# Layer 2's one-hots by nodes: four comparisons with a number per partition in place of one comparison of two tensors

## The chip, the cores and the metric

The kernel runs on one core of one Trainium2 chip. The metric is the time of one execution on the device in microseconds (us), the median over several runs. The engines of the core work side by side, each through its own queue in order: TensorE (PE; its weight loads are listed as PEld), VectorE (DVE), ScalarE (ACT), GpSimd (POOL) and SyncE (SP). They wait for each other through semaphores.

## The reference

A graph network of four layers over 12,500 nodes with 96 features and 200,000 edges sorted by destination. Each layer is added to its input and normalised. The change concerns layer 2, attention along the edges:

```python
Q_h = (x @ Wq + bq).reshape(N, H, D)          # H = 8 heads of D = 12
K_h = (x @ Wk + bk).reshape(N, H, D)
V_h = (x @ Wv + bv).reshape(N, H, D)
E = (edge_attr @ We + be).reshape(-1, H, D)
score = K_h[src_idx] * Q_h[dst_idx] / jnp.sqrt(jnp.asarray(D, x.dtype)) * E
score = jnp.exp(jnp.clip(score.sum(-1, keepdims=True), -5.0, 5.0))
msg = V_h[src_idx] * score
wV = jax.ops.segment_sum(msg, dst_idx, num_segments=N)
Z = jax.ops.segment_sum(score, dst_idx, num_segments=N)
h_out = wV / (Z + 1e-06)
...
x = _layernorm(x + h_out.reshape(N, H * D))
```

The two segment sums are what the changed lines serve: each edge's message and weight are added to the row of its destination node.

## The kernel before, in words

`passes()` does layers 0 and 1, `attention()` does layer 2, and a last `whole_pass` does layer 3, one after the other. Layer 3 reads a table of layer 2's result (`ex_d`, and `kept[2]` on the chip), so it starts when layer 2 has ended.

In `attention()` the 200,000 edges are 1563 tiles of 128 edges, an edge per partition. Four tiles are a unit (`UE` = 4), so there are 391 units, the last one of three tiles. Nodes are grouped in 98 windows of 128. Because edges are sorted by destination, a tile's edges fall into two neighbouring windows, `nominal(t)` and the next one; `by_columns` computes for each edge its node's place in these two windows, a number from 1 to 256 (`within`, one column per tile, lines 570 to 583).

Per unit the kernel does the following.

- `ask(u)`, line 1536: GpSimd issues four indirect DMAs, one per tile, that gather for each of 128 edges the row of K and V of its source (`kv_d`, 192 f32) into `kv`, a ring of 12 buffers. It is called 8 units ahead (`EARLY`). The indices are a column of `cols` on the chip. In what follows, "a gather" is one of these instructions.
- `queries(u)`, lines 1563 and 1564: ScalarE makes the one-hots that pick the destination's Q row.
- `score(u)`: TensorE multiplies the edge attributes by We (`ep`, line 1574) and picks Q (`qp`, line 1578). VectorE forms the products (1582, 1583), sums over each head (1585) and clips (1586).
- `weigh` and `terms`: ScalarE takes the exponential (1594, 1596), VectorE multiplies V by it (1597), and both split the f32 message into two f16 halves (1606 and 1607, tile `mh`).
- `one_hots_of(u)`, line 1613: VectorE compares `wide`, a table of the numbers 1 to 256 with each number repeated four times, with `within`, and so makes for the four tiles of the unit the 128 x 256 one-hot that says which edge goes to which node (`ohe`, bf16). The layout is node first, tile last: `ohe[p, node, tile]`.
- `scatter(u, m, ohe)`, line 1629: for each tile and each of its two windows TensorE multiplies a 128 x 128 slice of `ohe` as weights by the 208 columns of `mh` and accumulates in PSUM. When a window is complete, `done` (lines 1642 to 1647) divides by the sums, and after four windows a `stage` (lines 1655 to 1698) normalises the nodes and writes layer 3's table, a few instructions per unit.

The order on PE, DVE, ACT and POOL in this stage is the order in which the code calls these functions (`manual_schedule`): in the loop's turn u the score of unit u, the weighing of u - 1, the splitting and the one-hots of u - 2, the scatter of u - 3. On VectorE a turn is thus 1582, 1583, 1585, 1586, 1597, 1607, 1613, then the `done` and `stage` instructions that are due. Line 1613 waits for nothing but a free buffer; the next instruction, line 1582 of the following unit, waits for that unit's four gathers and for `ep`.

In layers 0 and 1 other lines are of use as a measure: 1013 is a VectorE comparison of a bf16 row with a number per partition, 1311 an indirect DMA of GpSimd like that of line 1536, 1018 a scan along a row.

Of the kernel before, what the change touches and what calls it, by code (L numbers as in the profile page):

```python
# [11 lines left out]
F32 = mybir.dt.float32  # L12
BF16 = mybir.dt.bfloat16
# [3 lines left out]
ALU = mybir.AluOpType  # L17
# [6 lines left out]
P = 128  # L24
# [496 lines left out]
NT = (E + P - 1) // P  # L521
# [20 lines left out]
def gnn_fast(  # L542
# [4 lines left out]
    nc = tc.nc  # L547
# [19 lines left out]
    nc.vector.memset(eps, LN_EPS)  # L567


    def by_columns(pool, t0, t1):  # L570

        cols = pool.tile([P, t1 - t0], I32, name="cols")
        nc.sync.dma_start(cols, cols_src[:, t0:t1])
        within = pool.tile([P, t1 - t0], BF16, name="within")
        with tc.tile_pool(name="n_work", bufs=1) as work:
            dst_i = work.tile([P, t1 - t0], I32, name="dst_i")
            nc.scalar.dma_start(dst_i, cols_dst[:, t0:t1])
            nom = work.tile([P, t1 - t0], I32, name="nom")
            nc.gpsimd.iota(nom, pattern=[[1, t1 - t0]], base=t0 + 8, channel_multiplier=0)
            nc.vector.tensor_scalar(nom, nom, 4, None, op0=ALU.arith_shift_right)  # L580
            nc.vector.tensor_scalar(nom, nom, P, -P - 1, op0=ALU.mult, op1=ALU.add)
            nc.vector.tensor_sub(within, dst_i, nom)
        return cols, within

    def without_slots(pool, ns):

        t0 = 16 * ns - 8
        src_, in_0 = by_columns(pool, t0, NT)
        in_1 = pool.tile([P, NT - t0], BF16, name="in_1")
        nc.vector.tensor_scalar(in_1, in_0, float(-P), None, op0=ALU.add)  # L590
        return ns, t0, src_, (in_0, in_1)
# [44 lines left out]
    with tc.tile_pool(name="w_work", bufs=2) as work, tc.tile_pool(name="w_psum", bufs=2, space=PSUM) as psum:  # L636
        for i in range(DEPTH):
            t = const.tile([D + 1, 2 * D], F32, name=f"w_l1_{i}")
# [72 lines left out]
    for i in range(2):  # L711
        t = const.tile([D + 1, GB, P], F32, name=f"aug{i}")
# [115 lines left out]
    def nominal(t):  # L828
        return (t // 8 + 1) // 2 - 1
# [666 lines left out]
    def attention():  # L1496
        H1 = HD + 1
        W = HEADS * H1
        per = UE
        EARLY = 8  # L1500
        with ExitStack() as c2:
            cols, within = by_columns(c2.enter_context(tc.tile_pool(name="e_cols", bufs=1)), 0, NT)
            work = c2.enter_context(tc.tile_pool(name="e_work", bufs=3))
            uw = c2.enter_context(tc.tile_pool(name="e_unit", bufs=3))
            one = c2.enter_context(tc.tile_pool(name="e_one", bufs=1))
# [1 line left out]
            accp = c2.enter_context(tc.tile_pool(name="e_acc", bufs=3, space=PSUM))  # L1507
            five = one.tile([P, per, HEADS], F32, name="five")
            nc.vector.memset(five, 5.0)
            wide = one.tile([P, 2 * P, per], BF16, name="wide")  # L1510
            nc.gpsimd.iota(
                wide, pattern=[[1, 2 * P], [0, per]], base=1, channel_multiplier=0, allow_small_or_imprecise_dtypes=True
            )
            attr = []
            for i in range(6):
                t = one.tile([D + 1, per * P], F32, name=f"attr{i}")
# [3 lines left out]
            blocks, got, asked, early, acc, held = {}, {}, {}, {}, {}, {}  # L1520
# [88 lines left out]

            def one_hots_of(u):  # L1610
                t0, n = units[u]
                o = uw.tile([P, 2 * P, per], BF16, name="ohe")
                nc.vector.tensor_tensor(  # L1613
                    o[:, :, :n], wide[:, :, :n], within[:, None, t0 : t0 + n].to_broadcast([P, 2 * P, n]), op=ALU.is_equal
                )
                return o

            def scatter(u, m, ohe):
                t0, n = units[u]
                for i in range(n):  # L1620
                    t = t0 + i
                    for k in range(2):
                        d = nominal(t) + k
                        if not 0 <= d < NB:
                            continue
                        first, last = max(0, 16 * d - 8), min(NT - 1, 16 * d + 23)
                        if t == first:
                            acc[d] = accp.tile([P, 2, W], F32, name="acc")
                        nc.tensor.matmul(  # L1629
                            acc[d].rearrange("p t w -> p (t w)"), ohe[:, k * P : (k + 1) * P, i],  # L1630
                            m[:, i].rearrange("p t w -> p (t w)"), start=(t == first), stop=(t == last),
                        )
                        if t == last:
                            done(d, acc.pop(d))

            def done(d, a):
                g = d - d % GB
                n = min(GB, NB - g)
                if d == g:
                    held["y"] = one.tile([P, GB, D], F32, name="y")  # L1640
                s = uw.tile([P, W], F32, name="both")
                nc.vector.tensor_reduce(s, a.rearrange("p t w -> p w t"), AX.X, ALU.add)
                sh = s.rearrange("p (h d) -> p h d", d=H1)
                z = uw.tile([P, HEADS, 1], F32, name="z")
                nc.vector.tensor_scalar(z, sh[:, :, HD:], 2.0**-8, 1e-6, op0=ALU.mult, op1=ALU.add)
                nc.vector.reciprocal(z, z)
                nc.vector.tensor_mul(
                    held["y"][:, d - g, :].rearrange("p (h d) -> p h d", d=HD), sh[:, :, :HD], z.to_broadcast([P, HEADS, HD])
                )
                if d == g + n - 1:  # L1650
                    stages.append(stage(g, n, held.pop("y")))
# [53 lines left out]
            with tc.manual_schedule(engines={ET.PE, ET.DVE, ET.Activation, ET.Pool}):  # L1705
                for u in range(EARLY):
                    ask(u)
                for u in range(3):
                    queries(u)
                for u in range(len(units) + 3):  # L1710
                    ask(u + EARLY)
                    fetch(u + 4)
                    if u < len(units):
                        steps[0].append(score(u))
                    if 1 <= u < len(units) + 1:
                        steps[1].append(weigh(*steps[0].pop(0)))
                    if 2 <= u < len(units) + 2:
                        steps[2].append((terms(*steps[1].pop(0)), one_hots_of(u - 2)))
                    queries(u + 3)
                    if stages and next(stages[0], stages) is stages:  # L1720
                        stages.pop(0)
                    if u > 2:
                        scatter(u - 3, *steps[2].pop(0))
                for st in stages:
                    for _ in st:
                        pass
# [90 lines left out]
    with tc.tile_pool(name="h_tab", bufs=1) as pool:  # L1817
        kept[2] = new_table(pool, 4 * D, F16)
        at_3 = without_slots(pool, NS3)
        attention()  # L1820
        whole_pass(
            at_3, ex_d, in_batches(l3_stage, terms=(2, 1, 1)), in_batches(l3_stage, terms=(2, 1, 1), name="sums_e"),
            kept[2][1],
        )


    with tc.tile_pool(name="f_work", bufs=1) as work, tc.tile_pool(name="f_psum", bufs=1, space=PSUM) as psum:
        t = work.tile([P, 1], F32, name="found")
# [3 lines left out]
        p = psum.tile([1, 1], F32, name="p")  # L1832
# [59 lines left out]
```

## Time and profile before

| | us |
|---|---|
| median of 3 runs | 5880.89 |
| lowest and highest run | 5874.62, 5888.94 |
| the profiled execution | 5885.37 |
| its span, first to last instruction | 5883.6 |
| layer 2, 2895 to 4993 | 2098 |
| layers 0 and 1, before it | 2895 |
| layer 3, after it | 891 |

| busy us in the span | PE | PEld | DVE | ACT | POOL |
|---|---|---|---|---|---|
| whole | 4446.7 | 3267.7 | 4378.5 | 2718.9 | 4095.9 |
| layer 2 | 1409.8 | 1276.9 | 1564.1 | 1012.2 | 1591.0 |

Durations are from the one profiled execution. A group of instructions is named by its line, its engine and its operation, then the tile that it writes and those that it reads, with the number of times, the busy time, the mean of one in ns, and how long its engine had been idle before it, with what ended that. "issue" means that nothing the profile shows was waited for. Two instructions of VectorE that follow each other without a wait overlap in these records by about 80 ns, so what one costs its queue is the distance between two starts.

### The profile page before, as it was taken

To read this page: it belongs to the slowest core of one execution; us is meant where nothing else is said; L and a number is where in the kernel's file an instruction comes from. 1 tells how busy PE (TensorE), PEld (TensorE's weight loads), DVE (VectorE), ACT (ScalarE), POOL (GpSimd) and SP (SyncE) were. 2 spreads that over 40 slices of the span, in tenths; PEclk is the share of its full clock that TensorE was granted. 3 is DMA by queue.
4 is the path that set the end of the run, shared out by engine and by line. 5 is a ranking of instruction groups with operands and counts; after the bars stand their busy time and mean duration, and the time that the engine had idled before them with its cause. 6 is when DMAs were issued, how large, how long until landed. Compare 5 with 4: busy or idle time off the path is not lost. (4 is left out here: it accounts for less than half of the span.)

```text
span 5883.6 us, 131235 instructions
## 1 busy us (share of the span) xinstructions
PE 4446.7 (76%) x51487; PEld 3267.7 (56%) x51487; DVE 4378.5 (74%) x9063; ACT 2718.9 (46%) x5380; POOL 4095.9 (70%) x3648
## 2 busy tenths in 40 slices
PE   4667777777778987898666667666666765899998
PEld 3444444554456765666566566666666664445454
DVE  7589899998746665776677777777777777577776
ACT  1445444444534443555444444444444444444444
POOL 0267677767667775777477777777777776777773
PEclk7576767776779998999755655555556566899999
DMA  3555555555556665776555555555555554555553
GB/s 100 156 156 184 172 170 173 164 166 166 179 149 167 171 160 140 190 193 187 150 152 155 157 156 156 156 156 155 156 153 156 155 157 131 137 145 151 146 151 88
DMA packets 671708, 920.46 MB, mean 156 GB/s; under 512 B 399034, under 2 KB 465293, under 8 KB 671077
## 3 DMA queue, kind: packets, MB, share of 16 engines
q1 hardware_dynamic: 502198, 621.59, 33.7%
q0 software_dynamic: 150624, 283.99, 20.8%
q10 hardware_dynamic: 18255, 6.39, 0.5%
q8 instruction: 406, 6.65, 0.5%
q14 instruction: 225, 1.84, 0.1%
HBM read 778.75 MB, written 132.81 MB: 155 GB/s over the span
## 5 line engine op out<-in xcount | busy, mean ns | idle before, releaser
L1311 POOL DMA_INDIRECT rows_e<-tab_d,cols x1257 | 1658.3, 1319 | 423.7 <-issue 292.9
L1536 POOL DMA_INDIRECT kv<-kv_d,cols x1563 | 1590.9, 1018 | 485.4 <-issue 382.0
L1369 ACT CAST msg<-rows 128x768 f16<-128x768 f32 (+1 forms) x1320 | 796.9, 640 | 853.8 <-PE rows L1366 832.8
L1629 PE MATMUL acc<-mh,ohe 128*128 128x208 f16 x3115 | 566.7, 355 | 661.3 <-DVE ohe L1613 653.8
L1369 DVE CAST msg<-rows 128x768 f16<-128x768 f32 x660 | 630.0, 955 | 369.5 <-PE rows L1366 363.6
L1629 PEld LDWEIGHTS <-ohe 128*128 128x128 bf16 x3115 | 379.3, 137 | 781.8 <-DVE ohe L1613 738.4
L1366 PE MATMUL rows<-tab,ohT 128*32 128x192 f16 (+1 forms) x19992 | 763.8, 277 | 56.0 <-ACT msg L1369 21.7
L1311 POOL DMA_INDIRECT rows_e<-ex_d,cols x611 | 592.2, 969 | 186.2 <-issue 154.2
L1375 PE MATMUL acc<-msg,ohd 128*128 128x192 f16 (+1 forms) x5100 | 693.7, 276 | 1.6 <-issue 1.6
L1574 PE MATMUL ep<-w_e,attr 97*128 97x96 f32 x3126 | 689.7, 396 | 5.0 <-DVE s L1582 4.2
L1574 PEld LDWEIGHTS ep<-w_e,attr 97*128 97x128 f32 x3126 | 660.4, 310 | 14.1 <-DVE s L1582 4.6
L1366 PEld LDWEIGHTS <-ohT 128*32 128x32 fp8e4 x19992 | 425.5, 97 | 350.8 <-issue 298.5
L1297 PE MATMUL acc<-rows_e,ones_e 128*128 128x192 f16 (+2 forms) x3660 | 493.3, 285 | 93.8 <-DMA rows_e<-tab_d,cols 51.2
L1582 DVE TENSOR_TENSOR s<-ep,kv 128x384 f32<-128x384 f32 x391 | 217.6, 556 | 442.8 <-DMA kv<-kv_d,cols 358.9
L1594 ACT ACTIVATE ex<-sc 128x32 f32<-128x32 f32 x391 | 89.6, 229 | 984.8 <-DVE sc L1586 951.8
L1375 PEld LDWEIGHTS <-ohd 128*128 128x128 fp8e4 x5100 | 407.0, 99 | 233.4 <-issue 179.3
L1235 ACT CAST msg<-rows 128x768 f16<-128x768 f32 x600 | 366.0, 641 | 319.0 <-PE rows L1231 293.0
L1297 PEld LDWEIGHTS <-ones_e 128*128 128x128 bf16 x3660 | 365.2, 117 | 187.9 <-issue 93.9
L1244 PE MATMUL acc<-msg,ohd 128*128 128x193 f16 x1800 | 305.1, 295 | 112.8 <-ACT msg L1235 100.6
L1231 PE MATMUL rows<-tab,ohT 128*32 128x192 f16 x7056 | 332.2, 294 | 49.6 <-ACT msg L1235 20.0
L1175 POOL DMA_INDIRECT spare<-tab_d,spare_i x72 | 141.5, 1966 | 317.8 <-DMA rowd<-lorow 134.9
L1018 DVE TENSOR_TENSOR_SCAN cnt<-cb,run,sb 128x2048 bf16<-128x2048 bf16 (+1 forms) x73 | 324.3, 4443 | 4.6 <-DMA cb<-crow 4.6
(701 smaller groups left out, 7577.7 us busy)
## 6 DMA issues: line engine op xcount, KB each, us to landing
ohT<-ohT_d SPq DMA_DIRECT2D x204, 400.0 KB
ohd<-ohd_d SPq DMA_DIRECT2D x204, 400.0 KB
attr<-cols_edge_attr_dram SPq DMA_DIRECT2D x390, 192.0 KB
bc<-rowd SPq DMA_DIRECT2D x72, 800.0 KB
qb<-qrow SPq DMA_DIRECT2D x97, 512.0 KB
sb<-srow SPq DMA_DIRECT2D x72, 512.0 KB
cb<-crow SPq DMA_DIRECT2D x72, 512.0 KB
ohd_d<-ohd SPq DMA_DIRECT2D x72, 400.0 KB
```

Of the source, the lines that this page charges most:

```text
L1018: nc.vector.tensor_tensor_scan(cnt[:, : n * P], cb[:, : n * P], sb[:, : n * P], c.run, op0=ALU.mult, op1=ALU.add)
L1231: nc.tensor.matmul(ps[j * GR : (j + 1) * GR, i // R, i % R * W : (i % R + 1) * W], a, b, start=True, stop=True)
L1235: nc.scalar.copy(m[:, : n * R, :W].rearrange("p (b r) w -> p b r w", r=R), ps[:, :n, : R * W].rearrange("p b (r w) -> p b r w", r=R),)
L1244: nc.tensor.matmul(acc[d][:, : W + 1], got[d][1][:, q, :], m, start=(q == 0), stop=(q == SQ - 1))
L1297: nc.tensor.matmul(acc[:, : W + count], ones[:, :, i], rows_of[u][:, i, : W + count], start=(t + i == first), stop=(t + i == last),)
L1311: nc.gpsimd.indirect_dma_start(out=m[:, i, :W], out_offset=None, in_=table, in_offset=bass.IndirectOffsetOnAxis(ap=rest_src[:, t : t + 1], ...
L1366: nc.tensor.matmul(ps[j * GR : (j + 1) * GR, i // R, i % R * W : (i % R + 1) * W], a, b, start=True, stop=True)
L1369: (nc.scalar.copy if engine else nc.vector.tensor_copy)(m, ps[:, :, : R * W])
L1375: nc.tensor.matmul(acc[d][:, :W], got[d][1][:, q, :], m, start=(q == 0), stop=(q == SQ - 1))
L1536: nc.gpsimd.indirect_dma_start(out=kv[:, i, :], out_offset=None, in_=kv_d, in_offset=bass.IndirectOffsetOnAxis(ap=cols[:, t0 + i : t0 + i ...
L1574: nc.tensor.matmul(ep[:, i, :], a[:, i * P : (i + 1) * P], w_e, start=True, stop=True)
L1629: nc.tensor.matmul(acc[d].rearrange("p t w -> p (t w)"), ohe[:, k * P : (k + 1) * P, i], m[:, i].rearrange("p t w -> p (t w)"), start=(t = ...
```

## The change

The one-hots of a unit are made by four instructions, one per tile, each comparing the table with one number per partition, the tile's column of `within`. The table holds each number once, the layout of `ohe` is tile first and node last, and `scatter` takes its weights from adjacent columns. `within` is kept in f32 in this layer. On TensorE's queue each tile's first weight load now waits for that tile's comparison; on the others the order is the same, but for a load of the node stage (`x_in`) that moves by a few places on SP's queue.

```diff
-    def by_columns(pool, t0, t1):
+    def by_columns(pool, t0, t1, dtype=BF16):
...
-        within = pool.tile([P, t1 - t0], BF16, name="within")
+        within = pool.tile([P, t1 - t0], dtype, name="within")
...
-            cols, within = by_columns(c2.enter_context(tc.tile_pool(name="e_cols", bufs=1)), 0, NT)
+            cols, within = by_columns(c2.enter_context(tc.tile_pool(name="e_cols", bufs=1)), 0, NT, F32)
...
-            wide = one.tile([P, 2 * P, per], BF16, name="wide")
-            nc.gpsimd.iota(
-                wide, pattern=[[1, 2 * P], [0, per]], base=1, channel_multiplier=0, allow_small_or_imprecise_dtypes=True
-            )
+            wide = one.tile([P, 2 * P], BF16, name="wide")
+            nc.gpsimd.iota(wide, pattern=[[1, 2 * P]], base=1, channel_multiplier=0, allow_small_or_imprecise_dtypes=True)
...
-                o = uw.tile([P, 2 * P, per], BF16, name="ohe")
-                nc.vector.tensor_tensor(
-                    o[:, :, :n], wide[:, :, :n], within[:, None, t0 : t0 + n].to_broadcast([P, 2 * P, n]), op=ALU.is_equal
-                )
+                o = uw.tile([P, per, 2 * P], BF16, name="ohe")
+                for i in range(n):
+                    nc.vector.tensor_scalar(o[:, i], wide, within[:, t0 + i : t0 + i + 1], None, op0=ALU.is_equal)
...
-                            acc[d].rearrange("p t w -> p (t w)"), ohe[:, k * P : (k + 1) * P, i],
+                            acc[d].rearrange("p t w -> p (t w)"), ohe[:, i, k * P : (k + 1) * P],
```

## The prediction

> **What bounds the kernel now.** I read the page first, for the whole; then the busy time by stage, to find the stage of the change; then the gathers' own line, for what their engine waits for; then the timeline, instruction by instruction.
>
> From the page, the costliest groups (count, busy us, mean ns, then the engine's idle time before them and what ended it):
>
> ```profile
> L1536 POOL DMA_INDIRECT kv<-kv_d,cols x1563 | 1590.9, 1018 | 485.4 <-issue 382.0
> ...
> L1629 PE MATMUL acc<-mh,ohe 128*128 128x208 f16 x3115 | 566.7, 355 | 661.3 <-DVE ohe L1613 653.8
> ...
> L1582 DVE TENSOR_TENSOR s<-ep,kv 128x384 f32<-128x384 f32 x391 | 217.6, 556 | 442.8 <-DMA kv<-kv_d,cols 358.9
> ```
>
> TensorE waits 654 us for the one-hots of L1613, which looks like the bound. It is not: VectorE, which makes them, itself stood idle 443 us at L1582, the first instruction of each unit, mostly for the gathered rows. The gathers are GpSimd's. Stage by stage (PE, PEld, DVE, ACT, POOL busy us, clock, DMA share, GB/s):
>
> ```profile
> 2895.00:4993.00 2098.00, 1409.80 (x9379) 1276.86 (x9380) 1564.11 (x3433) 1012.21 (x2131) 1590.95 (x1563) 0.59 0.56 155
> ```
>
> From the source view of the gathers' line:
>
> ```profile
> L1536 POOL DMA_INDIRECT kv<-kv_d,cols x1563: 942/949/1477, 2901.2 to 4967.4; - x196
> ...
>   issue: 382.0, 1253
>   DVE ohe L1613: 56.7, 186
> ```
>
> The first gather starts at 2901.2 and the last at 4967.4. 1590.9 us busy plus 1562 gaps of 0.305 us (382.0/1253, and 56.7/186 for those put down to L1613: the same length, so no real wait) is 1590.9 + 476 = 2067, which is that whole stretch. GpSimd issues gathers back to back and never waits for a buffer: it is the bound of this stage, at 4 x (1.018 + 0.305) = 5.29 us per unit.
>
> A gather usually takes 946 ns; the mean is 1018. The excess, 1563 x 72 ns = 113 us, is what can be won or lost here. The timeline shows it:
>
> ```profile
> 4006.12 0.58 DVE L1607 TENSOR_TENSOR mh<-m,mh 128x416 f16<-128x416 f32 x1
> 4006.62 0.69 DVE L1613 TENSOR_TENSOR ohe<-wide,within 128x1024 bf16<-128x1024 bf16 x1
> ...
> 4006.68 1.45 POOL L1536 DMA_INDIRECT kv<-kv_d,cols  x1 [0.30 <-issue]
> 4008.43 0.95 POOL L1536 DMA_INDIRECT kv<-kv_d,cols  x1 [0.30 <-issue]
> ```
>
> The gather that starts 60 ns into L1613 takes 1.45 us instead of 0.95. I set each of the 1563 gathers against the VectorE instruction running 34 ns after its start. With a comparison or product of two SBUF tensors there, the gather is longer by the rest of that instruction less 90 ns: for L1613, 103 gathers, 398 ns each measured and 398 by the rule; L1597, 180 of 206 (rule 207); L1607, 77 of 257 (rule 257). With nothing or a PSUM-fed instruction there, 711 gathers and more, about 2 ns. So L1613 costs 103 x 398 = 40.9 us, L1597 37.0, L1607 19.8, the node stage's lines the rest.
>
> **What the Trainium skill says.** "SBUF — State Buffer", Who interferes with whom: VectorE and GpSimd share one pair of SBUF ports; a VectorE instruction with two SBUF inputs collides with GpSimd's reads, one in a two-port mode with reads and writes. The trace agrees on reads (above). It says that the loser blocks for the whole instruction; here L1613 runs 675 to 739 ns beside gathers of 945, so it doesn't wait them out, and the measurement decides. "VectorE: DVE Perf Modes", The perf-mode tier table: bf16 tensor_scalar gets the fourfold, two-port mode, tensor_tensor twofold. The trace agrees: L1013, the same form as the new comparison (bf16, is_equal, a number per partition), takes 740 ns for 2048 elements, L1613 682 for 1024.
>
> **The change part by part.**
>
> *VectorE's time.* L1613 occupies the queue for about 600 ns (L1607 to L1613 is 502 ns apart for 416 elements, so 69 ns over one element per cycle at 0.96 GHz; 1024 at two per cycle is 533 + 67). A comparison of 256 elements: L1013's pair at 1150.82 starts 660 ns apart, 533 of it stream, so 127 fixed. L1053, with a number per partition, is 162 apart from its follower, and L1064, with a constant, 102: 60 ns are the scalar's. So 256/4/0.96 = 67 + 127 = 194 ns, four are 776: 176 ns more per unit.
>
> *Waits of VectorE for a gather.* L1661, a two-port instruction of 4 elements, takes 168 ns alone and 385 when it starts 555 ns after a gather; all such end about 940 ns after the gather's start. The gather thus holds the ports from about 590 to 840 ns. Four comparisons of 776 ns against 1250 ns of cycle: 0.2 x 125 + 0.62 x 250 = 180, and 20 for the gather's brief read: 0.2 us per unit. Together 0.38 us more per unit; VectorE is idle 1.13 us per unit at L1582 (442.8/391), so GpSimd stays the bound and this costs nothing but about 0.5 us in the drain after the last gather. If the idle time were gone, it would cost 147 us.
>
> *What goes from GpSimd:* L1613's blocks, -40.9 us.
>
> *What comes, reads.* A group lies in 776/5290 = 14.7% of the time: 229 gathers start their read in it. The ports are held some 0.45 of each 194 ns (67 ns of stream at least): 103 gathers. Each waits half of that, 44 ns, and may miss the gap behind. In layer 0, where VectorE runs port-holding instructions back to back, I count 43 of 157 such gaps missed; in layer 2's tensor_tensor chain none. 0.27 x 194 and its repeats are about 60. 103 x 104 ns = +10.7. Bounds: 229 x 0.35 x 33 = +3 (held for the 67 ns of stream alone, no gap missed) to 1563 x 0.147 x 388 = +89 (every gap missed).
>
> *What comes, writes.* L1613 never delayed a gather's descriptor writing; two-port instructions do. At 453.3 us L1013 starts 392 ns into a gather and ends (less 90) 1045 ns in: the gather takes 1255, so writing has to start by 740 ns. The same count is 103 gathers, but a hold that ends before 740 costs nothing: I take +6; bounds 0 and 1563 x (626/5290) x 313 = +58.
>
> *L1607's gap.* Behind it now stands a comparison with a scalar: 77 x 0.27 x 194 = +4 at most, taken +2.
>
> *At no cost.* The smaller table (iota, 2.26 us now at 1614.7) lies in GpSimd's 30 us wait before it. `within` in f32 is the same 1.78 us subtraction at 2896, beside a load of indices that GpSimd waits for until 2901. TensorE's weights from adjacent columns: its work per unit, 3.6 us, has 1.7 us of slack. A wait per matmul for its own comparison lets the first start earlier, with nothing behind it. SP's loads keep their work; the row load of the node stage moves a few places and is needed once per 16 units.
>
> *Sum.* -40.9 + 10.7 + 6 + 2 + 0.5 = -22 us. Profiled execution: 5885.4 (span 5883.6) becomes 5863; the median shown, 5880.9, is 4.5 below that execution, so **5859**. What is late next: L1597 and L1607 still block. Their shares move with the phase: if gathers met them at random, L1597 would cost 1563 x 400^2/(2 x 5290) = 24 and L1607 28, against 37 and 20 now; so +-15 besides.
>
> **The rivals.**
>
> A, forecast (0.50): gathers slip in between the comparisons: 5842 to 5868.
>
> B, given back (0.15): the phase throws more gathers onto L1597 and L1607, or a third more gaps are missed: 22 us shrink below 11.8, 5869 to 5892, say 5875. For it: L1597 and L1607 lie in every unit. Against: the random sum, 24 + 28 + 42, is near the measured 98.
>
> C, starved gathers (0.30): slower. GpSimd gets no port until the whole group is through, in place VectorE's L1613, with the price +89 + 58 - 41 = +106 us: 5987; with half of the blocks, +32, 5913. It decides from where a gather that meets the group (229 in reading, 185 in writing) loses over 128 ns on average, 53 us, against the 40 ns taken above and 355 for this rival in full. For it: at 845.65 a gather took 6.50 us, through two L1013 and a scan without a gap used. Against: at 1150.22 a gather of 1.47 us ended in the gap between two L1013.
>
> D, VectorE becomes the bound (0.05): needs 1.13 us more per unit, against 0.38 worked out. It would take comparisons without the fourfold mode (256/0.96 + 127 = 394 ns each, +0.98 us) and the waits all the same, +1.18: 5.34 us per unit, +20, 5901. Against: L1013's 740 ns.
>
> **How the numbers follow.** Predicted is A's 5859, its own range 5842 to 5868. Below 5838 I leave 0.05. Upwards the range takes in B, D and C to 5950, where two thirds of C lie: 5838 to 5950. Runs of this kernel spread by about 0.2% (5874.6 to 5888.9), so no change is within 11.8 us of 5880.9. Faster by more: A, 0.50. Same: B, 0.15. Slower: C and D, 0.35.
>
> **What would show it.** Right: the gathers' mean falls from 1018 to about 1004 ns, gaps still 0.305, four comparisons of some 275 ns each starting 194 apart, idle time at L1582 falling from 1.13 to about 0.75 us per unit, the last gather at about 4945. Wrong by C: a mean above 1018, gathers that end with the fourth comparison, 1.5 us and more. Wrong by D: gaps between gathers over 0.305 and no idle time at L1582.

## The result, and the profile after

| | before | after |
|---|---|---|
| median of 5 runs, us | 5880.89 | 5836.68 |
| lowest and highest run | 5874.41, 5888.94 | 5827.11, 5850.60 |
| the profiled execution | 5885.37 | 5850.6 |
| ratio, after to before | | 0.993, 95% interval 0.992 to 0.9941 |

The changed kernel is faster by 44 us between the medians (35 to 47 by the interval). The forecast was 22 us: the sign and the mechanism hold, the size is half of what came. The median of 5836.68 lies below the 5842 to 5868 of the forecast and 1.3 us below the lower end, 5838, of the whole range; the ratio, 0.993 of 5880.89, is 5840 and just inside it.

Line numbers of `attention()` move up: 1536 becomes 1534 (the gathers), 1582 becomes 1580, 1597 becomes 1595 (the product of the messages), 1607 becomes 1605 (the difference of the halves), 1613 becomes 1612 (the comparison), 1629 becomes 1626 (the scatter's matmuls). The page of after, the costliest groups:

```profile
L1534 POOL DMA_INDIRECT kv<-kv_d,cols x1563 | 1551.0, 992 | 485.0 <-issue 382.0
...
L1626 PE MATMUL acc<-mh,ohe 128*128 128x208 f16 x3115 | 569.9, 357 | 611.3 <-DVE ohe L1612 608.5
...
L1580 DVE TENSOR_TENSOR s<-ep,kv 128x384 f32<-128x384 f32 x391 | 217.4, 556 | 317.8 <-DMA kv<-kv_d,cols 258.0
```

The gathers are busy 39.9 us less than before (1590.9 to 1551.0), in the same number of instructions, with the same idle time between them (485.4 and 485.0). TensorE's wait for the one-hots is 45 us shorter (653.8 and 608.5). That is about as much as the time fell, so these two lines alone do not say which of the two is the cause; the experiments do. The source view of the gathers' line in after:

```profile
L1534 POOL DMA_INDIRECT kv<-kv_d,cols x1563: 942/946/1422, 2902.9 to 4928.9; - x196
...
  issue: 382.0, 1254
  DVE ohe L1612: 54.6, 179
```

The first gather starts 1.7 us later than before, the last 38.5 us earlier. Each gap is still 0.305 us (382.0/1254, 54.6/179), so GpSimd still never waits for a buffer. Busy time by stage (PE, PEld, DVE, ACT, POOL, clock, DMA share, GB/s), over the same window as shown of before:

```profile
2895.00:4993.00 2098.00, 1445.39 (x9603) 1280.23 (x9604) 1662.14 (x4626) 1021.56 (x2149) 1578.47 (x1592) 0.58 0.57 157
```

VectorE has 98 us more busy time in it than before, in a window that now also holds the first instructions of layer 3; it became busier and the kernel faster. The timeline of after, two neighbouring gathers:

```profile
4005.49 0.58 DVE L1605 TENSOR_TENSOR mh<-m,mh 128x416 f16<-128x416 f32 x1
4005.99 0.90 DVE L1612 TENSOR_SCALAR ohe<-wide,within 128x256 bf16<-128x256 bf16 x4
...
4005.24 1.15 POOL L1534 DMA_INDIRECT kv<-kv_d,cols  x1 [0.30 <-issue]
4006.70 1.01 POOL L1534 DMA_INDIRECT kv<-kv_d,cols  x1 [0.30 <-DVE ohe L1612]
```

The second gather starts inside the group of four comparisons and takes 1.01 us, where one that started inside L1613 took 1.45.

The same count as in the prediction, each gather against the VectorE instruction running 34 ns after its start, gives for the excess over 946 ns each (us in all):

| at the line of | before | after |
|---|---|---|
| the comparison | 40.9 (103 gathers) | 10.8 (164 gathers over 20 ns) |
| the product of the messages | 37.0 | 38.6 |
| the difference of the halves | 19.8 | 15.8 |
| the node stage and the rest | 14.6 | 7.2 |
| sum | 112.3 | 72.4 |

In six of the experiments' runs the kernel before, run beside them, itself took 7954 to 7959 us in place of 5881; their times are given but nothing about the theory is concluded from them, and only what their traces show of single gathers is used.

### The profile page after: what moved, and what is told of

Read it like the earlier page. It is cut to its first block, busy times and chain, and to the rows that moved or that the text cites. A ratio compares the mean times of both kernels' runs of the same rounds, so it can differ in the third digit from the quotient of the medians.

```text
span 5848.8 us, 132407 instructions
## 1 busy us (share of the span) xinstructions
PE 4460.3 (76%) x51487; PEld 3264.1 (56%) x51487; DVE 4463.2 (76%) x10235; ACT 2716.6 (46%) x5380; POOL 4042.8 (69%) x3648
## 5 line engine op out<-in xcount | busy, mean ns | idle before, releaser
L1534 POOL DMA_INDIRECT kv<-kv_d,cols x1563 | 1551.0, 992 | 485.0 <-issue 382.0
L1626 PE MATMUL acc<-mh,ohe 128*128 128x208 f16 x3115 | 569.9, 357 | 611.3 <-DVE ohe L1612 608.5
L1626 PEld LDWEIGHTS <-ohe 128*128 128x128 bf16 x3115 | 363.3, 131 | 748.9 <-DVE ohe L1612 691.1
L1580 DVE TENSOR_TENSOR s<-ep,kv 128x384 f32<-128x384 f32 x391 | 217.4, 556 | 317.8 <-DMA kv<-kv_d,cols 258.0
L1612 DVE TENSOR_SCALAR ohe<-wide,within 128x256 bf16<-128x256 bf16 x1563 | 359.7, 312 | 0.0
```

The costliest lines, as they stand in the source:

```text
L1534: nc.gpsimd.indirect_dma_start(out=kv[:, i, :], out_offset=None, in_=kv_d, in_offset=bass.IndirectOffsetOnAxis(ap=cols[:, t0 + i : t0 + i ...
L1612: nc.vector.tensor_scalar(o[:, i], wide, within[:, t0 + i : t0 + i + 1], None, op0=ALU.is_equal)
L1626: nc.tensor.matmul(acc[d].rearrange("p t w -> p (t w)"), ohe[:, i, k * P : (k + 1) * P], m[:, i].rearrange("p t w -> p (t w)"), start=(t = ...
```

## The experiments

The theory: GpSimd's gathers bound layer 2, and all that the change did to the time it did by lengthening fewer of them; what lengthens a gather is the rest of a VectorE instruction that reads two operands from SBUF, or of a comparison such as the new one, which lengthened 164 gathers though it reads one tensor and a number per partition. The rival: the gain comes from the one-hots' new layout, from weights that are ready tile by tile, or from VectorE's work.

**Two comparisons of 128 nodes, the layout of before.**

```diff
-                nc.vector.tensor_tensor(
-                    o[:, :, :n], wide[:, :, :n], within[:, None, t0 : t0 + n].to_broadcast([P, 2 * P, n]), op=ALU.is_equal
-                )
+                for c in range(0, 2 * P, 128):
+                    nc.vector.tensor_tensor(
+                        o[:, c : c + 128, :n], wide[:, c : c + 128, :n],
+                        within[:, None, t0 : t0 + n].to_broadcast([P, 128, n]), op=ALU.is_equal,
+                    )
```

> The kernel before with its one comparison cut into two of 128 nodes each: same operation, same layout, same operand types, same number of elements. Theory (a gather that starts while a VectorE instruction with two SBUF inputs runs waits out the rest of it): a gather loses about half the instruction's length, and the chance to fall into it goes with its length too, so the loss goes with the sum of squares: L1613's 41 us of lengthened gathers fall to about 21 us, and the time falls by about 20 us (0.996 to 0.997 of before). VectorE's work per unit grows by some 70 ns, which must cost nothing. Rival (the layout of the one-hots as weights of TensorE, or the time of VectorE, made the change faster): no gain, 1.000 or slightly above.

Measured: 5854.22 us against 5881.14, ratio 0.9954 (0.9941 to 0.9968). The excess at the comparison is 20.0 us, from 144 gathers of 139 ns (143 by the rule), as expected. The time fell by 27 us and not by 20: the other lines lost 9 us less too (71.4 to 62.1). The timeline shows one of the lengthened gathers:

```profile
3112.14 0.76 DVE L1614 TENSOR_TENSOR ohe<-wide,within 128x512 bf16<-128x512 bf16 x2
3112.17 1.21 POOL L1536 DMA_INDIRECT kv<-kv_d,cols  x1 [0.30 <-issue]
```

It starts as the first half does and waits for that half only (0.27 us), not for both. Cutting one instruction in two gave more than half of the change's gain, without its operation and without its layout. TensorE's weights are ready half by half here, so this run does not decide that part of the rival. It does speak of TensorE's wait:

```profile
L1631 PE MATMUL acc<-mh,ohe 128*128 128x208 f16 x3115 | 644.5, 361 | 531.9 <-DVE ohe L1614 521.4
```

The wait for the one-hots fell by 132 us (653.8 to 521.4), three times as much as in the changed kernel, and the time by less: that wait is not on the path.

**Four comparisons of 64 nodes, the layout of before.** The same diff with 64 in place of 128.

> As the one in halves, cut into four comparisons of 64 nodes each. Theory: L1613's 41 us of lengthened gathers fall to about 10 us, the time by about 30 us (0.994 to 0.996), although VectorE's comparisons then take about 0.8 us for each unit, 0.2 us longer than before. Rival (layout or time of VectorE): no gain, or a loss.

Measured: 5850.82 us, 0.9949 (0.9936 to 0.9963). The time is the expected one, but by luck: 25.6 us are left at the comparison instead of 10, and the other lines lost 54.9 in place of 71.4. The square law of the expectation for halves, in which the loss goes with the square of an instruction's length, fails here. 280 gathers fall on the group (against 144), and 11 of them lose over 50 ns more than the rest of their instruction, 7.0 us in all. In the timeline:

```profile
3126.75 0.89 DVE L1614 TENSOR_TENSOR ohe<-wide,within 128x256 bf16<-128x256 bf16 x4
3127.45 1.95 POOL L1536 DMA_INDIRECT kv<-kv_d,cols  x1 [0.30 <-DVE ohe L1614]
3127.56 0.55 DVE L1692 SCALAR_TENSOR_TENSOR mg<-mg,ex 128x384 f32<-128x384 f32 x1
3128.03 0.55 DVE L1693 TENSOR_TENSOR tab<-ex,tab 128x384 f16<-128x384 f32 x1
```

This gather began in the fourth comparison and waited through two more instructions with two SBUF operands, 1.0 us longer than usual. What lies between two such instructions is some 70 ns, and it is not always enough. Behind line 1692 eight more gathers of this kernel missed such a gap and lost 0.47 us each to it.

**Four comparisons of two tensors in the new layout.**

```diff
-            cols, within = by_columns(c2.enter_context(tc.tile_pool(name="e_cols", bufs=1)), 0, NT, F32)
+            cols, within = by_columns(c2.enter_context(tc.tile_pool(name="e_cols", bufs=1)), 0, NT)
...
-                    nc.vector.tensor_scalar(o[:, i], wide, within[:, t0 + i : t0 + i + 1], None, op0=ALU.is_equal)
+                    nc.vector.tensor_tensor(
+                        o[:, i], wide, within[:, t0 + i : t0 + i + 1].to_broadcast([P, 2 * P]), op=ALU.is_equal
+                    )
```

> The changed kernel in layout, count and order, but each of its four comparisons is again one of two tensors (the node number broadcast along the row, in BF16), which I expect to be as long as a quarter of unpaired elements, about 270 ns of streaming and 340 ns from one to the next, so 1.35 us for each unit. Theory (blocking by the comparison): four blocks of 270 ns in a row that merge nearly into one long one, with gaps of 70 ns in which a waiting gather gets through: 42 us or more of lengthened gathers at the comparison's line, and most of the gain is gone: 0.998 to 1.002 of before. Rival (the new layout, or that TensorE's weights are ready one by one, made the gain): 0.993 stays.

Measured: 5924.64 us, 1.0079 (1.0065 to 1.0093): slower than the kernel before, on the theory's side of the two but beyond the range that I expected of it. From its page:

```profile
L1534 POOL DMA_INDIRECT kv<-kv_d,cols x1563 | 1631.7, 1044 | 485.1 <-issue 372.1
...
L1628 PE MATMUL acc<-mh,ohe 128*128 128x208 f16 x3115 | 600.3, 356 | 634.2 <-DVE ohe L1612 632.4
...
L1612 DVE TENSOR_TENSOR ohe<-wide,within 128x256 bf16<-128x256 bf16 x1563 | 556.1, 417 | 0.0
```

The gathers' busy time is 40.8 us above that of before, and the time 43.5 us. The comparison costs 66.8 us (386 gathers of 173 ns); the difference of the halves, untouched, costs 52.1 instead of 19.8. This kernel has the layout, the count and the weights ready tile by tile of the changed one, so none of these made the gain; TensorE's wait is 21 us shorter than before and the time 43.5 us longer. It also shows that VectorE's length is not what counts: its four comparisons start 335 ns apart, 0.55 us more for each unit than in after, and the idle time between gathers is still 485.1.

**The one-hots made three times only.** The comparisons of the other 388 units are left out, so the scatter uses one-hots of other edges.

```diff
+            fixed = [one.tile([P, per, 2 * P], BF16, name=f"ohe{i}") for i in range(3)]
...
-                o = uw.tile([P, per, 2 * P], BF16, name="ohe")
+                o = fixed[u % 3]
+                if u > 2:
+                    return o
```

> The changed kernel with the one-hots made for the first three units alone and used again for all others: it leaves out the comparisons of the other 388 units. Theory (only what lengthens gathers counts): the comparisons still cost about 11 us in the changed kernel, so about 11 us below it (0.991 of before, 5820 to 5830 us), and VectorE's 0.78 us for each unit turns into idle time. Rival (VectorE's or TensorE's time in the stage is on the path): a fall of 100 us or more.

Measured: 5834.54 us, 0.9919 (0.9906 to 0.9933), above the 5820 to 5830 expected. From its page:

```profile
L1535 POOL DMA_INDIRECT kv<-kv_d,cols x1563 | 1545.3, 989 | 485.2 <-issue 386.6
...
L1629 PE MATMUL acc<-mh,ohe 128*128 128x208 f16 x3115 | 548.9, 349 | 653.3 <-DVE mh L1606 644.2
...
L1581 DVE TENSOR_TENSOR s<-ep,kv 128x384 f32<-128x384 f32 x391 | 217.7, 557 | 627.9 <-DMA kv<-kv_d,cols 578.7
```

Taking away all 1551 of these comparisons gains no more than the change itself, within the intervals. TensorE now waits as long for the split messages as it did for the one-hots, and what VectorE saves has become idle time (627.9 us). Their excess is gone, but the rest moved: 24.7 us at the product and 29.7 at the difference, the same 54.4 together as in after (38.6 and 15.8), and 12.3 elsewhere in place of 7.2. The rival, which puts VectorE's or TensorE's time on the path, expected 100 us or more and falls.

**ex in PSUM.** One operand of the product of the messages is moved, nothing else.

```diff
+            exp = c2.enter_context(tc.tile_pool(name="e_exp", bufs=1, space=PSUM))
...
-                ex = uw.tile([P, per, HEADS], F32, name="ex")
+                ex = exp.tile([P, per, HEADS], F32, name="ex")
```

It was run three times. The first two are among the six runs named above (8050.01 and 8057.99 us, ratios 1.0107 and 1.0152).

> The changed kernel with ex, the small operand of the product of the messages at L1595, put into PSUM, so that this product reads one operand from SBUF instead of two. Nothing else is touched. Theory (it takes two SBUF operands of a VectorE instruction to lengthen a gather): the 194 gathers lengthened at that line lose 38.6 us of lengthening, others shift by up to 10 us: 0.985 to 0.989 of before, about 5800 us. Rival (a gather is lengthened by any VectorE instruction of that length, whatever its operands): 0.992 to 0.994 as in the changed kernel.

> The kernel with ex in PSUM once more, since the chip of its first run took 7959 us for the kernel before (5881 in all other runs) with TensorE's instructions arriving late. Theory, where the kernel before takes about 5880 us: the layer's gathers are back to back, no gather is lengthened at the product of the messages, as the first run's trace already shows (49 gathers, 0 ns), and the 38.6 us lost there come off the changed kernel's time: 0.985 to 0.989 of before, about 5800 us. Rival (the gathers lengthened there shift to the other lines with two SBUF operands): 0.990 to 0.994.

> The kernel with ex in PSUM a third time, for a chip on which the kernel before takes about 5880 us. Theory: the stretch of the gathers is 1954.5 us plus what they are lengthened, and no gather is lengthened at the product of the messages: 25 to 45 us less than the changed kernel, 0.985 to 0.989 of before, about 5805 us. Rival (the lengthened gathers only shift to the other lines with two SBUF operands): 0.990 to 0.994.

In all six of those runs the kernel tried was slower than the kernel before beside it (ratios 1.0046 to 1.0191). In none of them are the gathers back to back, as the first run of ex in PSUM shows:

```profile
L1535 POOL DMA_INDIRECT kv<-kv_d,cols x1563 | 1514.5, 969 | 1026.2 <-DVE m L1596 583.7
```

GpSimd stood idle for 1026 us ahead of gathers in place of 485, 584 of them until VectorE's product had read the rows. So a shorter gather need not shorten the stage there. The changed kernel itself was not run beside these, so what it does then is not known.

Measured in the third: 5807.59 us against 5877.50, 0.9879 (0.9862 to 0.9895). That is the fastest kernel of this study, 29 us below the changed one. The lines are 1535 (gathers), 1596 (product), 1606 and 1613. Its page and its timeline:

```profile
L1535 POOL DMA_INDIRECT kv<-kv_d,cols x1563 | 1520.1, 973 | 485.0 <-issue 395.7
```

```profile
2937.05 0.55 DVE L1596 TENSOR_TENSOR m<-kv,ex 128x384 f32<-128x384 f32 x1
2937.14 0.95 POOL L1535 DMA_INDIRECT kv<-kv_d,cols  x1 [0.30 <-issue]
```

The gather starts 90 ns into the product, which is as long as ever (0.55 us), and takes its usual 0.95. Of 125 gathers that fall on this line, the excess is 0; in after, 194 cost 38.6 us. The rival of equal lengths falls. Of the 38.6 us, 31 were gained: the difference of the halves took some back (15.8 to 24.1). The time is inside the range expected.

**The number to compare with in PSUM, with the kernel before's one comparison.**

```diff
+            wip = c2.enter_context(tc.tile_pool(name="e_wi", bufs=1, space=PSUM))
...
+                wi = wip.tile([P, per], F32, name="wi")
+                nc.scalar.copy(wi[:, :n], within[:, t0 : t0 + n])
                 nc.vector.tensor_tensor(
-                    o[:, :, :n], wide[:, :, :n], within[:, None, t0 : t0 + n].to_broadcast([P, 2 * P, n]), op=ALU.is_equal
+                    o[:, :, :n], wide[:, :, :n], wi[:, None, :n].to_broadcast([P, 2 * P, n]), op=ALU.is_equal
                 )
```

> The kernel before, its one comparison of 1024 elements and its layout kept, but the four numbers by which it compares are copied by ScalarE into PSUM for each unit, in FP32, so that the comparison has one operand in SBUF and one in PSUM. I expect it to run at half the speed, about 1.1 us in place of 0.6. Theory (the pair of SBUF operands is what lengthens gathers): no gather is lengthened at the comparison's line and the 41 us go, with up to 10 us either way from other lines: 0.991 to 0.995 of before, although VectorE works 0.5 us longer for each unit. Rival (the gain of the change comes from its layout, from several short instructions, or from less of VectorE's work): 1.000 or slower.

> The kernel before with the comparison's numbers in PSUM once more, for the same reason. Theory, where the kernel before takes about 5880 us: the first run's trace shows no gather lengthened at the comparison (36 gathers, 0 ns) though it is longer; the 41 us that it costs in the kernel before go, with up to 15 us either way from the other lines: 0.991 to 0.996 of before. Rival (the gain needs the new layout or less work of VectorE): 1.000 or slower.

Both runs are among the six (7994.48 and 7994.17 us, 1.0046 and 1.0056), so the time expected of it stays untested. The timeline of the first shows what happens to a gather:

```profile
4061.13 1.21 DVE L1616 TENSOR_TENSOR ohe<-wide,wi 128x1024 bf16<-128x1024 bf16 x1
4061.83 0.95 POOL L1537 DMA_INDIRECT kv<-kv_d,cols  x1 [0.30 <-issue]
```

The comparison is nearly twice as long as L1613 was, 0.51 us of it were still to run, and the gather takes 0.95 us. Of 36 gathers on that line the excess is 0, where the rule would give 384 ns each; in the same trace 340 gathers at the difference of the halves, which is untouched, are longer by 178 ns each (181 by the rule). So at the level of one gather it is the second SBUF operand, not the length, the layout or the number of instructions.

**Two more kernels, also among the six runs.** One moves ex and m to PSUM (one buffer for both, and the next unit's weighing after this unit's terms), one adds three memsets of a small tile ahead of each unit's comparisons.

```diff
+            emp = c2.enter_context(tc.tile_pool(name="e_em", bufs=1, space=PSUM))
...
+                em = emp.tile([P, per * (W + HEADS)], F32, name="em")
+                ex = em[:, per * W :].rearrange("p (e h) -> p e h", h=HEADS)
...
+                m = em[:, : per * W].rearrange("p (e h d) -> p e h d", e=per, d=H1)
```

> As the last, with the message m in PSUM beside ex (one buffer for both), so that the difference at L1605 has one SBUF operand too; the order of a unit's steps changes: its terms and one-hots come ahead of the next unit's weighing. Theory: a further 15.8 us of lengthened gathers go: 0.982 to 0.986 of before, about 5785 us. Rival (the single buffer makes VectorE wait for ScalarE's Exp and its multiplication, some 0.8 us for each unit, as much as its idle time of 0.81 us): VectorE becomes the bound, 1.00 or above.

```diff
+                for _ in range(3):
+                    nc.vector.memset(pad, 0.0)
```

> The changed kernel with three small memsets of 96 elements ahead of each unit's four comparisons: about 0.5 us more of VectorE for each unit, 190 us in all, without an SBUF operand read. Theory (VectorE has 0.81 us of slack for each unit, and only what it reads as a pair costs): the time stays within 10 us of the changed kernel, 0.991 to 0.996 of before. Rival (VectorE's length of a unit sets the pace): 100 us or more above it.

Measured: 8117.41 us (1.0191) and 8032.12 us (1.0091), beside 7958.93. In the first one's trace the 52 gathers that fall on the difference of the halves have no excess where the rule would give 297 ns each, and the whole excess is 8.8 us. Whether its single buffer would make VectorE wait, and so be slower where the gathers are back to back, stays open. The time expected of the second is untested too; its question, VectorE's slack, is answered by the four comparisons of two tensors, which add more (0.55 us for each unit).

**The changed kernel again.**

> The changed kernel itself once more, because the last six kernels ran on two chips on which the kernel before takes 7954 to 7959 us in place of 5881: their traces show TensorE's instructions arriving late in all layers, and gathers that wait for VectorE behind it. If the chip is again like the first: 0.992 to 0.994 of before. If it is like the other two: theory, the gathers are no longer back to back there, so what lengthens them is no longer the bound, while a unit's VectorE work stands behind TensorE's late products and counts in full: 0.18 us more for each of 391 units is 70 us, 1.005 to 1.012 of before. Rival, the change gains there too: 0.99 to 0.998.

Measured: 5842.57 us against 5881.27, 0.993 (0.9916 to 0.9943), with 68.5 us of excess: 11.5 at the comparison, 36.7 at the product, 13.2 at the difference, 7.1 elsewhere. The split repeats within 3 us. The expectation's talk of two other chips is not upheld: one of those two later ran the kernel before at 5877.5 us (with the third run of ex in PSUM). What slowed the six runs stays open.

**All in one row.** The gathers' busy time (from each page) and the median time, as differences from the kernel before (its busy time from the one profile of it, its median from the runs beside the kernel in question):

| kernel | gathers' busy, us | difference | time's difference |
|---|---|---|---|
| changed kernel | 1551.0 | -39.9 | -44.2 |
| again | 1547.1 | -43.8 | -38.7 |
| halves | 1560.7 | -30.2 | -26.9 |
| quarters | 1559.1 | -31.8 | -30.3 |
| four of two tensors | 1631.7 | +40.8 | +43.5 |
| no comparisons | 1545.3 | -45.6 | -46.6 |
| ex in PSUM | 1520.1 | -70.8 | -69.9 |

Over a range of 113 us the two columns differ by at most 5.1 us, and the idle time between the gathers is 485.0 to 485.4 in all. What else these edits do reaches the time by no more than that.

## Why the prediction was right, and where its size was off

*The bound.* Right: gaps of 0.305 us in after too, and the table above. That TensorE's 654 us of waiting was no bound is shown by three kernels in which it and the time part: halves (wait -132, time -27), four comparisons of two tensors (wait -21, time +44) and no comparisons, where it became a wait of 644 us for something else.

*L1613's blocks, -40.9.* Right: they go with the instruction, and the kernel in halves shows them shrink with its length.

*New reads, +10.7.* Measured 10.8, but the agreement is luck, two errors that cancel: not 103 gathers of 104 ns but 164 of 66. More gathers meet the group (306, not 229; 199 of them fall on its fourth comparison), 54% of them find it in the way and not 45%, and none of them misses a gap. The charge of 27% of gaps missed came from layer 0 and was wrong here: no gather that meets the comparisons loses over 50 ns more than the rest of its instruction. Gaps are missed elsewhere in after, five times, between two instructions of the node stage that both read two operands from SBUF:

```profile
4214.89 0.55 DVE L1687 SCALAR_TENSOR_TENSOR mg<-mg,ex 128x384 f32<-128x384 f32 x1
4215.31 1.42 POOL L1534 DMA_INDIRECT kv<-kv_d,cols  x1 [0.30 <-issue]
4215.36 0.55 DVE L1688 TENSOR_TENSOR tab<-ex,tab 128x384 f16<-128x384 f32 x1
```

This gather had only some 2 ns of line 1687 to wait for by the rule, and lost 470 ns, the rest of line 1688. The five cost 2.4 us of the 7.2 in the table's line for the node stage; before has none.

*New writes, +6.* Mis-sized: 0. In after 280 gathers (those that began to read inside the group left out) had a comparison running in the stretch in which the prediction has them write, 590 to 840 ns in (later by what the gather had lost in reading), and none took over 20 ns more than the rule for its reading gives. It is the comparisons that wait there: 572 of the 1563 took over 300 ns, up to 451, where the middle one takes 279.

*L1607's gap, +2.* Mis-sized: 0. The 68 gathers there took 232 ns each, 234 by the rule.

*The other lines' phase, 0 with +-15 besides.* The largest term that was mis-sized: -9.9. The product and the difference together lost 54.4 in place of 56.8, the node stage and the rest 7.2 in place of 14.6. The second profile of after has 49.9 and 7.1, so this isn't chance of one execution. It lies inside the 15 us either way that I left for it, but I had taken it as zero on average; why the phase settles there was not shown, and the other kernels show how far it can go (75.9 at the two lines with four comparisons of two tensors).

*The sum.* -40.9 + 10.8 - 9.9 = -40.0, against 2067.1 us from the first gather's start to the last one's end before and 2026.9 after. In place of the -22 predicted the three mis-sized terms give 18 more, which is all but 4 us of the 44 between the medians; runs of one kernel spread by more than that. The profiled pair differs by 34.8 only because what lies ahead of and behind the gathers came out 5.5 us longer in that execution; the second profiled execution, 5841.68, is 43.7 below.

*VectorE.* The comparisons start 196 ns apart (194 predicted). The 0.96 elements per ns of the prediction come out of the runs: whole, in halves and in quarters the comparison of two bf16 tensors starts 602, 335 and 202 ns ahead of what follows it, so 512 elements take 267 ns and 256 take 133, at two per cycle, and some 69 ns are fixed. From the end of the instruction ahead of it to its own end the group takes 840 ns on average, L1613 took 603: 237 more, of which 56 are beyond four times 196. The waits for gathers thus cost 0.06 us per unit, not 0.2; where the first comparison waits (it ends 286 ns after its predecessor on average), the second makes most of it up (133 ns after the first). Idle time at the unit's first instruction is 0.81 us per unit (317.8/391), close to the 0.75 predicted, and again by two errors: VectorE's work grew by 0.24 us and not by 0.38, but the unit itself became 0.10 us shorter (40 us in 391 units), where the 0.75 left it as it was. That it costs nothing is right, and the four comparisons of two tensors show that 0.55 us more would still cost nothing by itself.

*The Trainium skill's two places.* "SBUF — State Buffer", Who interferes with whom, says that VectorE with two SBUF inputs collides with a GpSimd instruction that reads SBUF, and that with at most one, outside the two-port modes, it doesn't. The kernels with an operand in PSUM agree: 125 and 36 gathers, 0 ns. It says too that the first to start holds the pair for its whole instruction; in the kernel in quarters a gather lost 1.0 us behind instructions that began after it did, so a gather does not hold the pair from its start, and the measurement decides. "VectorE: DVE Perf Modes", The perf-mode tier table, gives the new comparison the fourfold mode: 196 ns apart agrees with the 194 worked out for it; at two elements per cycle the same working gives 260.

*The rivals.* C, starved gathers, had its point at 128 ns lost per gather that meets the group; measured are 35 in reading (10.8 us over 306 gathers) and none in writing. A loss of C's size can come about in another way: with four comparisons of two tensors, which stream for 0.27 us each in place of 0.07, the kernel was slower than before, though gathers there lose the rest of one comparison (173 ns each) and not of the whole group. B, more loss at the product and the difference, did not happen in after (54.4 us in place of 56.8); in that same kernel it did (75.9). D has no trace in the runs: no gap between two gathers is over 0.32 us.

## What to carry to other kernels

When GpSimd issues gathers back to back, price each VectorE instruction by what it does to them, and not by its share of VectorE's time: what counts here is whether it reads two operands from SBUF (or is of the new comparison's form) and how long one such instruction runs. One operand in PSUM took the loss at a line to nothing, and a comparison of 1.21 us with one operand in PSUM lengthened none of 36 gathers. Look first whether the gathers are back to back at all, then at their mean duration against their usual one; here that one number gave the time of seven kernels within 5.1 us. Treat the loss at other lines as something that moves when one line changes: removing all comparisons gained no more than shortening them.

## What the runs showed of the hardware that was not expected

- A gap of some 70 ns between two VectorE instructions with two SBUF operands is usually enough for a waiting gather, but not always: with comparisons of 64 nodes 11 of 280 gathers went on waiting, four of them for 1.0 us, and in after five did so in the node stage, for 0.47 us.
- The comparison of two bf16 tensors runs 533 ns of stream for 1024 elements, and cut into quarters it starts every 202 ns; with the number repeated along the row (four of two tensors) a quarter starts every 335 ns, with an operand in PSUM in FP32 the whole takes 1211 ns (682 before). The form of the operands set the speed by a factor of two.
- The pattern in which gathers meet VectorE's instructions is not random. In after 199 of 306 fall on the fourth comparison; with four comparisons of two tensors 341 of 386 fall on the third and fourth.
